# Last image of a four-layer vision block: half of its gate and output projection moved beside its scans, its first-layer input kept on the chip, filter products with wide weight tiles, ScalarE's copies shared

## The chip, the cores and the metric

The kernel runs on one core of a Trainium2 chip. The metric is the device time of one launch in microseconds (us). The engines named in what follows are TensorE (PE; its weight loads are listed as PEld), VectorE (DVE), ScalarE (ACT), GpSimd (POOL), and SyncE (SP), which issues the transfers; one queue of SyncE carries nearly all of them. SBUF is the memory on the chip with 128 partitions, PSUM the banks that TensorE writes into.

## The reference

Four images of 64 x 64 pixels with 96 channels pass through four layers, in float32 except where the feed-forward parts round to a small float format:

```python
x = x + mamba(group_norm(x))        # layer 0
x = depthwise_pointwise_conv(x)     # layer 1 (ReLU first, batch norm last)
t = tokens(x)                       # 4096 tokens of 96 channels
t = t + attention(ln(t))            # layer 2: six heads, no softmax
t = t + ffn(ln(t))                  # 96 -> 384 -> 96, rounded
t = t + filter(ln(t))               # layer 3
t = t + ffn(ln(t))

def mamba(x):
    xp, z = split(x @ W_in.T)                   # 192 channels each
    xc = silu(conv3x3(xp) + conv_b)
    # the same sequence by rows, by columns, and both reversed
    xs = four_orders(xc)
    dts, Bs, Cs = x_proj(xs)                    # 16 states
    delta = softplus(dt_proj(dts) + dt_b)
    # h = exp(delta*A)*h + delta*u*B ; y = sum(h*C) + D*u
    y = selective_scan(xs, delta, A, Bs, Cs, D)
    yy = y[0] + y[1] + y[2] + y[3]              # back in one order
    return (yy * silu(z)) @ W_out.T

def filter(x):
    h = relu(bn(x @ w1.T))                      # 96 -> 192
    X = fft(h, axis=tokens)                     # 4096 points
    xr = relu(X.real * rd - X.imag * id + rb)   # per channel
    xi = relu(X.imag * rd + X.real * id + ib)
    return bn(ifft(xr + 1j * xi).real @ w2.T)   # 192 -> 96
```

## The kernel before, in words

Channels lie on partitions and the 4096 positions of an image along the row, in eight blocks of 512. The kernel has a head, a scan stage and a tail.

**The head** (group norm, input projection and the 3 x 3 convolution of image 0) fills the inputs of the first scans. All such inputs go to DRAM tensors: step size, input product, B and C of the scans, `ud_s` (four times D times u) and `sz_s` (the gate, SiLU of z).

**The scan stage** has 192 phases: four images, each with two orientations (rows, columns), each with 24 groups of 8 channels x 16 states = 128 partitions. A phase takes one group through both directions in four chunks of 1024: ScalarE makes the decay (L1345), GpSimd multiplies by B (L1335), VectorE does four forward scans (L1568), four backward scans (L1611) and four adds (L1618), GpSimd multiplies by C (L1339), TensorE sums over the states (`py`, L1355), ScalarE copies (L1363), and the result goes to `y_s` in DRAM. For the column orientation ScalarE turns the inputs and the results by strided copies (L154) in a scratch tile `side`. The order within this stage is written out by hand. Eight times a phase `pieces` (L1421) gives pieces of other work to the engines, from two lanes. One lane has the scan inputs of images 1 to 3 and then `rest` of images 0 to 2; the other has the turns and `post` of images 0 to 2. Every piece states its cost on (PE, ACT, POOL, DVE, queue) in us; each step adds credit for each engine, and a piece goes out when there is credit for it.

**`post`** (L467) makes the first residual. For each block and each half of the 192 channels it loads three terms (the row result, `ud_s`, the turned-back column result), adds them in PSUM by products with the identity (`p_y`, L519), multiplies by the gate on VectorE (L494), projects by `w_out` (`p_out`, L546; two halves in one sum), adds x (L551), applies ReLU (L555) and stores `x1` to DRAM. For image 3 it runs after the last scan, with all eight PSUM banks.

**`rest`** (L698) has layers 1 to 3 of one image: `layer1` (nine taps, `p_l`, L753, from `x1` in DRAM), norms (`p_mean` L794, `p_var` L779, `p_rstd` L841), attention, a feed-forward, the filter, the last feed-forward (`p_f`, L960; copy L951, bias L953). Its argument `deep` is 1 beside the scans and 2 for image 3, which gives more buffers. Beside the scans the order is by hand; behind them the framework's scheduler orders what the lanes give, and helpers such as `evacuate` alternate between ScalarE and VectorE.

**The filter** writes the 4096 points as 64 x 64 and does the FFT as two steps of products with tables. `filter_in` (L1002) works on thirds of 64 channels. `p_h` (L1030) takes 64 columns of `ln`, every 64th element, as weights against `w1s`; it does each product twice, to partitions 0 to 63 and 64 to 127, so that both halves hold the same result. The gate `hb` (L1014) applies ReLU and a diagonal mask, and `p_dft` (L1051) takes 64 columns of `hb` at the same spacing against the real and the imaginary table, again in two column halves. The result `z` goes to DRAM (`z_s`) and comes back with other axes on the partitions. `filter_mid` (L1070) has 16 rounds of four frequencies: `p_dft2a` (L1107) with two thirds in two column halves, `p_dft2b` (L1116) with the last third, ReLU copies `ya` and `yb`, and the projection by `w2a` and `w2b` (`p_o`, L1090 and L1091). `filter_turn` (L1154) and `filter_out` (L1193) do the inverse.

The order of the tail is thus `post` of image 3, `layer1`, norm, attention, norm, feed-forward, norm, `filter_in`, `filter_mid`, `filter_turn`, `filter_out`, norm, feed-forward and output.

Of the kernel before, what the change touches and what calls it, by code (L numbers as in the profile page):

```python
# [10 lines left out]
F32 = mybir.dt.float32  # L11
# [7 lines left out]
NB = 4  # L19
# [54 lines left out]
def layers(ctx: ExitStack, tc: tile.TileContext, a: dict, out):  # L74
# [99 lines left out]
    def turn_back(side, b):  # L174

        yield from until(lambda: ("columns", b) in done)
        yield from turn(side, halves_of(y_s[1][b], y2_s[b]))

# [51 lines left out]
    def group_norm(wk, take, images, ready):  # L230
# [5 lines left out]
        for k, b in enumerate(images):  # L236
            stats = wk.tile([C, NBLK, 6], F32, tag="stats", name="stats", bufs=2)
            for i in range(NBLK):
                xs = wk.tile([C, BLK], F32, tag="xs", name="xs", bufs=4)
                nc.sync.dma_start(xs, a["xT"][:, b * L + i * BLK : b * L + (i + 1) * BLK])  # L240
                nc.vector.bn_stats(stats[:, i, :], xs)
                if i % 2 == 1 and n > 1:
                    yield NEXT
# [24 lines left out]
    def before_scans(b, wk, take, deep=1, prev=None):  # L268
# [109 lines left out]
        def k2(name, rows=C):  # L378
            return wk.tile([rows, BLK], F32, tag=name, name=name, bufs=2 * deep)

        soft = []
# [85 lines left out]
    def post(place, take, b, ahead):  # L467
# [3 lines left out]
        yield from until(lambda: ("scans", b) in done)  # L471

        def load(name, src, k):
            i, c = divmod(k, 2)
# [23 lines left out]
        def add_up():  # L498

            held = []  # L500
            for k in range(2 * NBLK):
# [22 lines left out]
                if k + 1 + ahead < 2 * NBLK:  # L524
                    yield (0, 0, 0, 0, 2.4)
                    nxt.append(load_terms(k + 1 + ahead))
                if k + 1 < 2 * NBLK and (k == 0 or k - 1 in used):
# [5 lines left out]
        for i in range(NBLK):  # L533
# [5 lines left out]
            for c in range(2):  # L539
                yield from until(lambda: 2 * i + c in sums)  # L540
                if c == 0:
                    p, give = yield from take("p_out")
                y, since = sums.pop(2 * i + c)
                yield from steps_past(since, 1)
                yield (0.9, 0, 0, 0)
                nc.tensor.matmul(p, lhsT=w_out[:, c, :], rhs=y, start=(c == 0), stop=(c == 1))  # L546
                used.add(2 * i + c)
# [6 lines left out]
            yield (0, 0.63, 0, 0, 1.6)  # L554
            nc.scalar.activation(xr, xr, AF.Relu)  # L555
            store(x1[b][:, cols], xr)
            yield NEXT
            flush()
            done["x1", b] = i + 1


    ident = mean_w = centre = pick = head_mask = dft1 = idft1 = taps = l1s = wk_a = wv_a = wqT = None
    bq = wff = bff = ffn2 = ffn3 = w1s = filt = imp = w2a = w2b = s2 = None

    def constants(wk, take, ready):

        nonlocal ident, mean_w, centre, pick, head_mask, dft1, idft1, taps, l1s, wk_a, wv_a, wqT
        nonlocal bq, wff, bff, ffn2, ffn3, w1s, filt, imp, w2a, w2b, s2
# [95 lines left out]
        w2a = const("w2a", [128, C], a["w2T"][0:128, :], cb)  # L664

        w2b = cb.tile([128, 2, C], F32, tag="w2b", name="w2b")
        nc.vector.memset(w2b, 0.0)
        for k in range(2):
            nc.sync.dma_start(w2b[k * N1 : (k + 1) * N1, k, :], a["w2T"][128:DI, :])
# [24 lines left out]

    def add_to(dst, src):
        (nc.gpsimd if ordered[0] else nc.vector).tensor_tensor(dst, dst, src, ALU.add)

    def rest(b, take, deep):  # L698
# [8 lines left out]
        def layer1(wk):  # L707
            x3 = x1[b].rearrange("p (r w) -> p r w", w=HW)

            def load(i):  # L710
                r0, lo, hi = rows_of(i)
                x = wk.tile([C, RPB + 2, HW], F32, tag="x", name="x", bufs=2)
# [51 lines left out]
        def layernorm(wk, hold, dst, source, result, previous=None):  # L764
# [3 lines left out]
            def half_of(h):  # L768
# [12 lines left out]
                def centred(i, pm, give):  # L781
# [3 lines left out]
                    nc.scalar.copy(hold[:, blk(i)], pm)  # L785
# [44 lines left out]
                def scale(i, pr, give):  # L830
                    kept = {} if dst.dtype == F32 else {"saturate": False}
                    nc.vector.tensor_tensor(dst[:, blk(i)], hold[:, blk(i)], pr, ALU.mult, **kept)  # L832
                    give(True)
                    ready[result] = i + 1
# [102 lines left out]
        def feed_forward(wk, weights, q, source, result, write=None):  # L937
# [4 lines left out]
            engine = nc.gpsimd if ordered[0] else nc.vector  # L942

            def first():
                for i in range(NBLK):
# [4 lines left out]
                    def out_of(j, p, give):  # L950
                        nc.scalar.copy(y[:, j, :], p)  # L951
                        give()
                        nc.scalar.activation(  # L953
                            y[:, j, :], y[:, j, :], AF.Relu, bias=b1[:, j : j + 1]
                        )
# [13 lines left out]
                    engine.tensor_copy(h, y, saturate=False)  # L969
                    hs[i] = h  # L970

            def second():
                for i in range(NBLK):
# [13 lines left out]
                    nc.scalar.copy(z, p)  # L987
                    give()
                    nc.scalar.activation(z, z, AF.Identity, bias=b2)
                    engine.tensor_tensor(t[:, blk(i)], t[:, blk(i)], z, ALU.add)  # L990
# [11 lines left out]
        def filter_in(wk, ln):  # L1002

            ln3 = ln.rearrange("p (n1 n2) -> p n1 n2", n2=N1)

            def third(hc):
                hs = slice(hc * N1, (hc + 1) * N1)
                yield from until(lambda: count("hb") >= hc)

                hb = wk.tile([128, N1, N1], F32, tag="hb", name="hb")  # L1010
                z = wk.tile([128, N1, N1], F32, tag="z", name="z")
# [11 lines left out]
                for k in range(8):  # L1023
                    p, give = yield from take("p_h", 128, held=held)
                    p = p.rearrange("p (n h) -> p n h", h=N1)
                    for j in range(8):
                        if j % 4 == 0:
                            yield (1.3, 0, 0, 0)
                        for at in (0, N1):
                            nc.tensor.matmul(  # L1030
                                p[at : at + N1, j, :], lhsT=ln3[:, :, 8 * k + j], rhs=w1s[:, hs],
                                start=True, stop=True,
                            )
                    yield from settle(held)
                    held.append(((0, 0, 0, 0.7), gate, (k, p, give), clock[0]))
                yield NEXT
                yield from settle(held)

                def out_of(k, p, give):
                    evacuate(z[:, :, 8 * k : 8 * k + 8], p.rearrange("p h k -> p k h"))  # L1040
# [3 lines left out]
                for k in range(8):  # L1044
                    p, give = yield from take("p_dft1", 128, held=held)
                    p = p.rearrange("p (h k) -> p h k", k=N1)
                    for j in range(8):
                        if j % 4 == 0:
                            yield (1.3, 0, 0, 0)
                        for ri in range(2):  # L1050
                            nc.tensor.matmul(  # L1051
                                p[ri * N1 : (ri + 1) * N1, j, :], lhsT=hb[:, :, 8 * k + j],
                                rhs=dft1[:, ri, :], start=True, stop=True,
                            )
# [6 lines left out]
                for q in range(4):  # L1061
                    yield (0, 0, 0, 0, 2.1)
                    nc.sync.dma_start(
                        z_s[b][:, hc, chunk(q)], z.rearrange("p k c -> p (k c)")[:, chunk(q)]
                    )

            for hc in range(3):
                yield from third(hc)
# [676 lines left out]
```

## Time and profile before

The median is 6014.21 us, of three runs from 6010.89 to 6023.8. The profiled execution spans 6031.1 us.

| engine | busy us | share of the span | instructions |
|---|---|---|---|
| TensorE, products | 4284.0 | 71% | 19506 |
| TensorE, weight loads | 1848.1 | 31% | 19506 |
| VectorE | 4864.0 | 81% | 3492 |
| ScalarE | 3283.7 | 54% | 4452 |
| GpSimd | 4077.9 | 68% | 1961 |

By stretches of the span (busy us):

| stretch, us | what | PE | PEld | VectorE | ScalarE | GpSimd |
|---|---|---|---|---|---|---|
| 0 to 360 | head | 322.3 | 121.4 | 34.2 | 197.8 | 80.0 |
| 360 to 5469 | scans | 3475.2 | 1424.3 | 4696.0 | 2920.9 | 3991.2 |
| 5469 to 5543 | `post` of image 3 | 62.7 | 21.3 | 15.9 | 5.6 | 6.0 |
| 5543 to 5731 | `layer1` to first feed-forward | 164.9 | 58.2 | 43.6 | 88.2 | 0.6 |
| 5731 to 5847 | `filter_in` | 113.1 | 112.5 | 25.4 | 7.2 | 0 |
| 5847 to 5861 | way of `z` through DRAM | 3.2 | 2.8 | 1.0 | 0.6 | 0 |
| 5861 to 5916 | `filter_mid` | 54.3 | 50.1 | 12.7 | 11.4 | 0 |
| 5916 to 6031 | turn, inverse, norm, last feed-forward | 88.4 | 57.5 | 35.3 | 52.1 | 0 |

A row is read against its own length: an engine that is busy for nearly the whole stretch bounds it. Products and weight loads of TensorE overlap, so the two columns do not add up. PEclk in the lines of the profile is the granted clock of TensorE as a share of full speed; it differs between stretches, and so does the time of one product.

### The profile page before, as it was taken

How to read it: one execution, taken by the hardware profiler on the slowest of the kernel's cores; microseconds unless marked ns; L12 is line 12 of the kernel's file. 1: busy time of each engine (PE TensorE's matmuls, PEld its weight loads, DVE VectorE, ACT ScalarE, POOL GpSimd, SP SyncE). 2: the span in 40 equal slices, each digit the busy share in tenths (PEclk: the TensorE clock that was granted, in tenths of full speed). 3: DMA queues.
4: the chain of work that ended last, by engine and by line, in shares of the span. 5: the costliest groups of instructions: out<-in, count | busy, mean ns of one | idle time of the engine just before them, and what ended most of it. 6: DMA issues, size and time to landing. Idle time of an engine off the chain costs nothing. (4 is left out here: it accounts for less than half of the span.)

```text
span 6031.1 us, 64385 instructions
## 1 busy us (share of the span) xinstructions
PE 4284.0 (71%) x19506; PEld 1848.1 (31%) x19506; DVE 4864.0 (81%) x3492; ACT 3283.7 (54%) x4452; POOL 4077.9 (68%) x1961
## 2 busy tenths in 40 slices
PE   8978888889855774654577756675577566657888
PEld 3322222223211120343412203551122044512285
DVE  2058898898899899998899999999989999993222
ACT  4557767776663357555454465455435645461503
POOL 1268897898897668777677787777767877782000
PEclk9988888888866765566657755685776557757787
DMA  3268878876788868789978677786875588854021
GB/s 100 75 165 232 238 199 231 242 230 196 207 246 233 221 193 224 215 232 252 251 211 227 178 201 215 212 246 187 233 203 162 169 234 235 231 163 130 4 82 56
DMA packets 467624, 1170.28 MB, mean 194 GB/s; under 512 B 90240, under 2 KB 155372, under 8 KB 467180
## 3 DMA queue, kind: packets, MB, share of 16 engines
q1 hardware_dynamic: 467276, 1166.17, 69.6%
q8 instruction: 154, 2.52, 0.2%
q14 instruction: 194, 1.59, 0.1%
HBM read 1010.63 MB, written 155.19 MB: 193 GB/s over the span
## 5 line engine op out<-in xcount | busy, mean ns | idle before, releaser
L1339 POOL TENSOR_TENSOR S<-S,rep 128x1024 f32<-128x1024 f32 x768 | 1811.1, 2359 | 942.1 <-DVE S L1618 863.3
L1345 ACT ACTIVATE pa<-dl,nega 128x1024 f32<-128x1024 f32 x1344 | 1500.3, 1118 | 1470.1 <-DVE S L1618 1121.8
L1335 POOL TENSOR_TENSOR B<-B,rep 128x1024 f32<-128x1024 f32 x768 | 1795.0, 2366 | 73.7 <-DMA B<-duT_s 50.6
L1568 DVE TENSOR_TENSOR_SCAN S<-pa,S,B 128x1024 f32<-128x1024 f32 x576 | 1352.6, 2348 | 261.8 <-ACT pa L1345 67.6
L1611 DVE TENSOR_TENSOR_SCAN pa<-pa,edge,B 128x1024 f32<-128x1024 f32 x576 | 1354.4, 2351 | 66.8 <-ACT pa L1345 66.7
L1355 PE MATMUL py<-S,red 128*32 128x512 f32 x3072 | 632.9, 890 | 820.1 <-POOL S L1339 746.2
L359 PE MATMUL p_conv<-xp,conv_w 96*96 96x504 f32 (+3 forms) x2304 | 1059.9, 615 | 14.9 <-ACT u L372 12.9
L1618 DVE TENSOR_TENSOR S<-S,pa 128x1024 f32<-128x1024 f32 x768 | 932.1, 1214 | 6.6
L359 PEld LDWEIGHTS p_conv<-xp,conv_w 96*96 96x96 f32 x2304 | 387.2, 171 | 673.4 <-issue 619.0
L1568 DVE TENSOR_TENSOR_SCAN S<-pa,B 128x1024 f32<-128x1024 f32 x192 | 438.1, 2282 | 178.9 <-ACT pa L1345 178.4
L1611 DVE TENSOR_TENSOR_SCAN pa<-pa,B 128x1024 f32<-128x1024 f32 x192 | 440.9, 2296 | 5.4
L1355 PEld LDWEIGHTS py<-S,red 128*32 128x32 f32 x3072 | 76.0, 128 | 1189.3 <-POOL S L1339 972.2
L154 ACT COPY side<-side 96x256 f32<-96x256 f32 (+1 forms) x448 | 281.7, 629 | 62.3 <-DMA duT_s<-side 28.8
L794 PE MATMUL p_mean<-t,centre 96*96 96x512 f32 x256 | 207.3, 929 | 118.0 <-ACT sq L786 46.9
L753 PE MATMUL p_l<-x,taps 96*96 96x504 f32 (+3 forms) x576 | 268.9, 623 | 16.0 <-DMA x<-x 16.0
L1051 PE MATMUL p_dft<-dft,hb 128*64 128x64 f32 x3072 | 231.3, 320 | 59.4 <-DVE hb L1014 59.4
L1030 PE MATMUL p_h<-w1s,ln 97*64 97x64 f32 x3072 | 233.6, 342 | 35.2 <-DVE ln L832 20.6
L1030 PEld LDWEIGHTS p_h<-w1s,ln 97*64 97x64 f32 x3072 | 227.7, 251 | 79.3 <-issue 33.3
L1051 PEld LDWEIGHTS p_dft<-dft,hb 128*64 128x64 f32 x3072 | 227.2, 251 | 79.7 <-DVE hb L1014 63.0
L451 POOL TENSOR_TENSOR r<-r,lg 96x512 f32<-96x512 f32 x64 | 81.3, 1271 | 250.0 <-ACT lg L436 249.9
L1363 ACT COPY ys<-py 128x512 f32<-128x512 f32 x384 | 221.8, 578 | 22.4 <-PE py L1355 19.8
L841 PE MATMUL p_rstd<-rs_y,pick 32*96 32x512 f32 x256 | 169.5, 1004 | 70.4 <-DVE ln L832 23.6
(192 smaller groups left out, 5081.9 us busy)
## 6 DMA issues: line engine op xcount, KB each, us to landing
B<-du_s SPq DMA_DIRECT2D x768, 256.0 KB
dl<-delta_s SPq DMA_DIRECT2D x768, 256.0 KB
B<-duT_s SPq DMA_DIRECT2D x768, 256.0 KB
dl<-deltaT_s SPq DMA_DIRECT2D x768, 256.0 KB
z_s<-z SPq DMA_DIRECT2D x48, 512.0 KB
zl<-z_s SPq DMA_DIRECT2D x64, 384.0 KB
side<-y_s SPq DMA_DIRECT2D x96, 192.0 KB
rep<-bc_s SPq DMA_DIRECT2D x64, 256.0 KB
```

The source lines that it names most:

```text
L154: nc.scalar.copy(o.rearrange("p (w h) -> p w h", h=HW), t[:n, :].rearrange("p (h w) -> p w h", w=HW)[:, q * w : (q + 1) * w, :],)
L359: nc.tensor.matmul(pr[:, ra:rb, ca_:cb_], lhsT=conv_w[:, kc, ky * 3 + kx, oc * C : (oc + 1) * C], rhs=xp[:, kc, at + ra : at + rb, ca_ + d ...
L753: nc.tensor.matmul(p3[:, ra:rb, ca_:cb_], lhsT=taps[:, ky * 3 + kx, :], rhs=x[:, at + ra : at + rb, ca_ + dx : cb_ + dx], start=(k == 0), ...
L1030: nc.tensor.matmul(p[at : at + N1, j, :], lhsT=ln3[:, :, 8 * k + j], rhs=w1s[:, hs], start=True, stop=True,)
L1051: nc.tensor.matmul(p[ri * N1 : (ri + 1) * N1, j, :], lhsT=hb[:, :, 8 * k + j], rhs=dft1[:, ri, :], start=True, stop=True,)
L1335: nc.gpsimd.tensor_tensor(Bs[n, q], Bs[n, q], reps[n // NG, 0, q], ALU.mult)
L1339: nc.gpsimd.tensor_tensor(Ss[n, q], Ss[n, q], reps[n // NG, 1, q], ALU.mult)
L1345: nc.scalar.activation(pa, dls[n, q], AF.Exp, scale=nega[:, g : g + 1])
L1355: nc.tensor.matmul(py[32 * j : 32 * j + 32, :], lhsT=red, rhs=Ss[n, q][:, k * BLK : (k + 1) * BLK], start=True, stop=True,)
L1568: nc.vector.tensor_tensor_scan(s, pa, Bs[n, q], Ss[n, q - 1][:, CH - 1 : CH] if q else 0.0, ALU.mult, ALU.add)
L1611: nc.vector.tensor_tensor_scan(pa[:, ::-1], pa[:, ::-1], Bs[n, q][:, ::-1], edge if k else 0.0, ALU.mult, ALU.add,)
L1618: nc.vector.tensor_tensor(Ss[n, q], Ss[n, q], pa, ALU.add)
```

## The change

It has four parts.

1. *Half of gate and projection beside the scans.* The channels 0 to 95 of the last image have all four scan results once group 12 of its last orientation is through. So the side lane gets, at its end, a `post` of this half alone (`halves=(0,)`), whose result (with x, before ReLU) is stored to `x1`. For the channels 96 to 191 `sum_up` adds `ud_s` and the turned-back column results in advance and stores the sum to `ud_s`. The last phase loads these sums, the gates and the partial `x1` into tiles that the scans no longer need (`last_loads`). Behind the scans `last_post` loads only the row results of the upper half, adds, gates, projects, adds and applies ReLU.
2. *`x1` of the last image kept on the chip.* `last_post` writes it into the scratch tile `side`, and `layer1` reads it there. `side` is now allocated from the start, and some tiles of the head (`xs`, and `w`, `lg` of image 0) use its space.
3. *Filter products of 128 weight columns.* In the tail `ln` is written twice, side by side (the copy on GpSimd), so that `p_h` is one product with 128 weight columns and writes both halves at once. `p_dft` takes a pair of columns of `hb` as 128 weight columns against both tables side by side (128 moving columns), for all images. The thirds of the tail's `filter_in` are given to the scheduler as three parallel streams with two sets of buffers. `z` gets another layout; `filter_mid` loads it by four transfers a round and takes 96 weight columns of two half sets, 16 bytes from one to the next, each for all its channels; `ya`, `yb` are replaced by two tiles of 96 partitions, and the projection has two products with 96 rows for each frequency.
4. *Copies shared in the tail.* In the feed-forward parts copies and biases alternate between ScalarE and VectorE (`evacuate`, `plus_bias`); the copy `hold` of a norm goes to VectorE; the cast to eight bits goes to GpSimd.

The core of the diff:

```diff
+            if 1 in halves:
+                yield (0, 0.63, 0, 0)
+                nc.scalar.activation(xr, xr, AF.Relu)
...
+    def sum_up(place, take, b):
...
+            p, give = yield from take("p_sum", C, held=held)
+            yield (1.6, 0, 0, 0)
+            for j, x in enumerate(terms):
+                nc.tensor.matmul(p, lhsT=ident[:C, :C], rhs=x, start=(j == 0), stop=(j == 1))
...
+    def last_post(place, take, x1t):
+        b = NB - 1
+        for i in range(NBLK):
+            nc.sync.dma_start(place("y_in", i), y_s[0][b][C:, i * BLK : (i + 1) * BLK])
+        for i in range(NBLK):
+            cols = slice(i * BLK, (i + 1) * BLK)
+            y, w, sz, xr = (place(name, i) for name in ("y_in", "w_in", "sz_in", "xr"))
+            (nc.gpsimd if i % 2 else nc.vector).tensor_tensor(y, y, w, ALU.add)
+            nc.vector.tensor_tensor(y, y, sz, ALU.mult)
+            p, give = yield from take("p_out")
+            nc.tensor.matmul(p, lhsT=w_out[:, 1, :], rhs=y, start=True, stop=True)
+            nc.vector.tensor_tensor(xr, p, xr, ALU.add)
+            give()
+            nc.scalar.activation(x1t[:, cols], xr, AF.Relu)
...
+    def plus_bias(x, bias, relu=False):
+        if ordered[0] or not flip[0]:
+            nc.scalar.activation(x, x, AF.Relu if relu else AF.Identity, bias=bias)
+        elif relu:
+            nc.vector.tensor_scalar(x, x, bias, 0.0, ALU.add, ALU.max)
+        else:
+            nc.vector.tensor_scalar(x, x, bias, None, ALU.add)
...
+                    if result == "ln_s" and deep > 1:
+                        nc.gpsimd.tensor_copy(
+                            dst[:, L + i * BLK : L + (i + 1) * BLK], dst[:, blk(i)]
+                        )
...
-                        nc.scalar.copy(y[:, j, :], p)
+                        evacuate(y[:, j, :], p)
...
-                    engine.tensor_copy(h, y, saturate=False)
+                    nc.gpsimd.tensor_copy(h, y, saturate=False)
...
-                        for at in (0, N1):
+                        for at in (0,) if deep > 1 else (0, N1):
                             nc.tensor.matmul(
-                                p[at : at + N1, j, :], lhsT=ln3[:, :, 8 * k + j], rhs=w1s[:, hs],
-                                start=True, stop=True,
+                                p[at : at + deep * N1, j, :], lhsT=ln3[:, :, 8 * k + j],
+                                rhs=w1s[:, hs], start=True, stop=True,
...
-                        for ri in range(2):
-                            nc.tensor.matmul(
-                                p[ri * N1 : (ri + 1) * N1, j, :], lhsT=hb[:, :, 8 * k + j],
-                                rhs=dft1[:, ri, :], start=True, stop=True,
-                            )
+                    for j in range(4):
+                        nc.tensor.matmul(
+                            p[:, j, :], lhsT=pairs[:, :, 4 * k + j], rhs=table,
+                            start=True, stop=True,
+                        )
...
-                        for hc in range(2):
+                        for j in range(4):
                             nc.tensor.matmul(
-                                pa[hc * N1 : (hc + 1) * N1, j, :], lhsT=z[:, hc, j, :],
-                                rhs=tw[:, j, :], start=True, stop=True,
+                                p[:, j, :], lhsT=z[:, c, :, j], rhs=tw[:, j, :],
+                                start=True, stop=True,
                             )
...
+            if n == N - NG // 2 + 1:
+                done["half", NB - 1] = True
...
+    x1t = side[:, :L]
+    drain([*lanes, Lane(iter([([last_post(last_place, take, x1t)], [])]))])
```

## Prediction, made before the changed kernel had run

> **What bounds the kernel now.** I read the busy time by stretches first, then the chain of work that ended last, then the groups of instructions by line, and last the weight loads of the lines that the change rewrites.
>
> ```profile
> core 0: us, PE busy (x) PEld busy (x) DVE busy (x) ACT busy (x) POOL busy (x), PEclk, DMA share, GB/s
> 4500.00:5200.00 700.00, 448.09 (x2976) 237.96 (x2978) 660.94 (x464) 371.27 (x496) 531.68 (x247) 0.66 0.74 205
> 5455.00:5530.00 75.00, 63.60 (x135) 21.40 (x136) 27.18 (x31) 7.19 (x10) 9.91 (x5) 0.80 0.67 195
> 5650.00:5750.00 100.00, 79.69 (x390) 33.38 (x388) 33.08 (x48) 61.98 (x113) 0.00 (x0) 0.66 0.00 1
> 5750.00:5850.00 100.00, 94.44 (x1284) 93.84 (x1282) 20.52 (x31) 7.17 (x12) 0.00 (x0) 0.85 0.13 50
> 5850.00:5940.00 90.00, 81.28 (x1024) 76.62 (x1024) 16.70 (x30) 15.59 (x30) 0.00 (x0) 0.92 0.41 134
> ```
>
> There are two regimes. From 360 to 5469 us VectorE is full (94% in the first stretch shown): every phase has eight scans and four adds, 24.4 us in phases without other VectorE work. What VectorE gets besides lengthens a phase one for one; TensorE has room. From 5469 to 6031 (562 us) image 3 is alone and TensorE carries it, with its weight loads as busy as its matmuls where the filter products run.
>
> ```profile
> 5469.20 2.35 POOL S L1339
> ...
> 5543.15 48.92 PE p_l L753 x108
> ...
> 5731.40 18.91 PE p_h L1030 x253
> 5751.08 18.92 PE p_dft L1051 x256
> ...
> 5860.65 1.98 PE p_dft2a L1107 x16
> 5865.47 1.02 PE p_dft2a L1107 x16
> 5868.88 1.02 PE p_dft2a L1107 x16
> ...
> 5915.82 24.04 PE p_idft L1154 x384
> ```
>
> This is the chain: start, length, work. The tail divides into: gate and projection, 5469 to 5543 (74 us); first layer, norms, attention and feed-forward to 5731; `filter_in`, three times 18.9 + 18.9, 115.5 us; the way of `z` through memory to 5860.6; `filter_mid`, 16 rounds of 3.42, 55 us; the rest to the end.
>
> ```profile
> L1051 PEld LDWEIGHTS p_dft<-dft,hb x256: 217/251/257, 5751.1 to 5769.6; 128*64 128x64 f32 x128
> L1107 PEld LDWEIGHTS p_dft2a<-tw,zl x182: 132/137/137, 5872.2 to 5910.0; 128*64 128x64 f32 x182
> L1090 PEld LDWEIGHTS p_o<-w2a,ya x96: 186/192/192, 5870.3 to 5909.3; 128*128 128x128 f32 x96
> L154 ACT COPY side<-side x448: 607/624/1035, 396.1 to 5031.5; 96x256 f32<-96x256 f32 x128, 32x256 f32<-32x256 f32 x22
> ```
>
> Durations are minimum, median, maximum in ns. A load of 64 columns that lie side by side takes 132, of 128 such columns 186: (186 - 132) / 64 = 0.84 ns a column on 78 fixed. The same 64 columns taken 256 bytes apart (`p_dft`) take at least 217: 139 / 64 = 2.2 ns a column. ScalarE shows the same kind of thing: 624 ns for 256 elements read 256 bytes apart.
>
> [...] two passes of `p_dft`, one in each half of the columns, start 7 ns apart and a pair comes every 147 ns; between `p_dft2a` (two tiles) and `p_o` (one) lie about 0.2 us, twice a round.
>
> So the old pairs already used both halves of the array. What a single tile of 128 spaced columns costs, no row shows. Bounds: packed, 112 ns a pass (the step of `p_o`); at 2.2 ns, 128 x 2.2 + 6 = 287. The single records tell more: where the last load of a burst runs on after its partner, it shortens by about 0.2 ns per ns alone (lead 98 ns: 229 instead of 251), so a stream alone needs about 2.2 / 1.2 = 1.8 ns a column, and not half of 2.2. Sharing one supply would have shortened it by nearly the whole lead. With 1.67 to 1.84 a pass is 218 to 240; I take 228.
>
> **The change part by part.**
>
> *Half of gate and projection beside the scans; `x1` on the chip.* The eight gates and eight adds of the lower 96 channels move into the last phases: 16 x 0.68 = 10.9 us of VectorE, which is full there. The order of instructions puts 236.4 us of such side work before the end of the scans instead of 228.3 (+8; four casts of image 2 slip behind). `sum_up` costs VectorE nothing (16 products, 8 ScalarE copies of 0.58, 24 transfers, beside the scans). More transfers in the queue of the loads: +2. Scans: +10. Behind the scans, before: 74 us to the first `p_l`. After: product 2.4, `py` 2.0, copy 0.6, store and load back 6: first inputs 11 us after the scans, all eight by 18. VectorE then has 4 adds, 8 products and 8 adds, 20 x 0.69 = 13.8. But the order also leaves four to five blocks of image 2's last feed-forward here, ahead of `p_l` in TensorE's queue: 4 casts, 9 copies and 8 biases, 13 us more on VectorE. 27 us of VectorE from the end of the scans with a few us of waits: `p_l` at +30 instead of +74, so -44. From there `p_l` is bound by TensorE as before.
>
> *ScalarE's copies shared.* A feed-forward block costs ScalarE 4.35 us now (steady, no gaps):
>
> ```profile
> L953 ACT ACTIVATE y<-y,b_L 128x512 f16<-128x512 f16 x48 | 33.2, 737 | 0.0
> L951 ACT CAST y<-p_f 128x512 f16<-128x512 f32 x48 | 26.7, 598 | 10.3 <-PE p_f L960 10.3
> ```
>
> These are groups of the tail: busy, mean ns, idle before. After, ScalarE has half (2.2) and VectorE two copies (1.38), two biases on 16-bit data (no row; between 0.3, at the rate of the cast `h<-y`, 0.62 ns an element, and 0.69), the add (0.69), and in the last layer the scaling (0.68): about 3.5. The cast goes to GpSimd, 1.46 for 0.96, beside the next block. 8 x 0.85 = 7 for the last layer, and 1 from its norm: -8. In the second layer norms are interleaved [...]: -10. The copy of `ln` on GpSimd (bounded by its 1.27 for a two-input product of that size) lags VectorE's 0.68 over four blocks: +3 before `p_h` can start.
>
> *`filter_in`.* Of `p_h` 64 x 2 = 128 passes a third instead of 128 pairs: 128 x 0.228 = 29.2 us for 18.9. Of `p_dft` 32 x 2 = 64 passes: 14.6 for 18.9. Three thirds: 131.4 + 4 for the waits that stay (the order still runs `p_h` and `p_dft` of a third one after the other) = 135 for 115.5: +19. Images 0 to 2 change only `p_dft`, in TensorE's room: nothing.
>
> *`filter_mid`.* Eight products of 96 columns, 16 bytes apart, in 16 passes: 96 x 1.75 + 5 = 173 ns [...]. I take 170: 2.7 us; `p_o` stays at 16 x 0.112 = 1.8[...]. 4.5 for 3.42, over 16 rounds: +17. Four loads for one: +1 before the first round; the bytes are the same, 655 KB a round, beside 4.5 us.
>
> *Head.* `xs`, `w`, `lg` only change place: 0, hidden by TensorE's 161 of 180 us there.
>
> Sum: +10 - 44 - 8 - 10 + 3 + 19 + 17 + 1 = -12, so 6002 from 6014; I say 6000.
>
> **The rivals.**
> A. *A column 16 bytes from the next costs no more than a packed one.* For it: nothing measured[...]. `filter_mid` then +2 instead of +17: 5985. 0.17.
> B. *One wide tile loads spaced columns at near the packed rate.* Then `p_h` and `p_dft` take 112 to 150 ns a pass: 69 to 90 us for 115.5, and the tail wins about 55 more than I say: 5930. For it: two streams together deliver a column every 1.1 ns. Against it: the lone loads at the end of the bursts. 0.12.
> C. *Slower: the wide load keeps 2.2 ns a column, or the scans pay more.* 287 a pass: 192 x 3 x 0.059 = 34 more than I have. Or TensorE's fuller rounds and the five transfers a round hold up the scans, 20 us or more: SyncE issues a load in about 0.54 us, and 64 more per image stand before the loads of the scans; the planner books 0.9 for four `p_dft` products that take 1.8. Against it: phases 80 to 86 and 124 to 139 of before show next to no wait besides VectorE's own work. 6035. 0.16.
>
> **How the numbers follow.** My case, 0.55, spreads over 5985 to 6018: 218 or 240 a pass moves it by -6 and +7, biases and waits behind the scans by 8, the scans by 8. Range 5940 to 6035: it leaves out a good part of B and the upper part of C, under 0.2 together. Faster by over 0.2% (below 6002): about half of my case, A and B: 0.58. Slower (over 6026): 0.17. The same: 0.25.
>
> **What would show it.** Right: the first `p_l` about 30 us behind the last scan; weight loads of `p_h` near 300 ns where now 217 to 257 stand; `p_h` at 29 us and the tail's `p_dft` at 15 us a third; rounds of `filter_mid` at 4.5 us; last feed-forward blocks near 3.5 us apart; scans longer by about 10 us. Wrong: `p_h` under 20 us a third (B), rounds of 3.6 (A), `p_h` over 35 or scans longer by over 25 (C).

## The result, and the profile after

The changed kernel takes 6096.76 us (median; 6092.45 to 6110.99) where the kernel before takes 6018.26 beside it. The ratio is 1.0135, with a 95% interval of 1.0114 to 1.0157: it is slower by about 80 us. The forecast was 6000, faster, with a range up to 6035.

The stretches of the changed kernel (start and end, length, then busy time and number of instructions of PE, PEld, DVE, ACT and POOL, granted clock, share of the transfer engines, GB/s):

```profile
360.00:5543.00 5183.00, 3502.95 (x13337) 1451.37 (x13337) 4700.05 (x3205) 2908.54 (x3854) 3969.46 (x1874) 0.71 0.77 215
5543.00:5593.00 50.00, 29.75 (x57) 8.75 (x55) 36.61 (x43) 15.24 (x25) 28.07 (x18) 0.57 0.21 63
5593.00:5767.00 174.00, 151.66 (x459) 56.15 (x457) 70.55 (x114) 62.84 (x106) 18.96 (x23) 0.89 0.01 3
5767.00:5895.00 128.00, 126.28 (x576) 125.90 (x576) 25.56 (x39) 7.16 (x12) 0.00 (x0) 0.65 0.08 33
5905.00:5979.00 74.00, 74.00 (x512) 73.95 (x510) 14.89 (x23) 13.40 (x24) 0.00 (x0) 0.98 0.45 131
6029.00:6090.00 61.00, 40.92 (x98) 12.49 (x96) 37.98 (x61) 28.63 (x48) 12.66 (x8) 0.67 0.09 26
```

The tail, from the end of the last scan on, is 547 us where it was 563: shorter, as forecast. The scan stage, from the first scan to the end of the last, is 5186 us where it was 5107, with VectorE as busy as before (4700 against 4696 us). So VectorE does not have more to do there; it waits. These are two single executions: that of the kernel before took 15 us more than its median, that of the changed kernel 4 us less. So between these two profiles the scan stage is 79 us longer and the whole only some 60, while the medians differ by 79; by the medians the scan stage's excess is nearer 95 us. 79 is used below. The chain of the tail (start, length, work):

```profile
5592.75 47.89 PE p_l L834 x108
...
5798.57 14.08 PE p_dft L1141 x64
5812.65 27.85 PE p_h L1119 x128
5840.50 14.08 PE p_dft L1141 x64
...
5912.75 2.85 PE p_dft L1204 x16
5915.60 1.76 PE p_o L1186 x16
```

A third of `p_h` takes 27.85 us (18.9 before), a third of `p_dft` 14.08 (18.9), a round of `filter_mid` 2.85 + 1.76 = 4.61 (3.42). The weight loads behind these numbers (minimum, median, maximum in ns):

```profile
L1141 PEld LDWEIGHTS p_dft<-dft,hb x768: 291/313/316, 2501.0 to 5893.6; 128*128 128x128 f32 x192
L1204 PEld LDWEIGHTS p_dft<-tw,zl x1024: 250/274/284, 2696.1 to 5975.1; 128*96 128x96 f32 x171
```

The wide loads cost about what the forecast took: 14.08 / 64 = 220 ns a pass (I took 228), 2.85 / 16 = 178 (I took 170).

For the scan stage I set each phase against its content: 24.39 us for the scans and adds, the measured VectorE side work, and the rest as stall. Summed over 191 phases, side work grew from about 320 to 328 us (+8, the number of the forecast), and stalls from about 106 to 177 (+71). The new stalls lie in three places: phases 78 to 99 (filter of image 0), 124 to 141 (image 1), and from 168 to the end (image 2, and the new half). The waits of ScalarE on filter products over the scan stage show how they come about, first before the change, then after (engine, what waited, for what: us in total, times, longest):

```profile
ACT z L689 <- PE p_dft L1051: 64.2, 49, 4.5
ACT os L689 <- PE p_o L1091: 42.0, 26, 4.5
ACT ya L689 <- PE p_dft2a L1107: 20.7, 16, 3.0
```

```profile
ACT z L758 <- PE p_dft L1141: 76.0, 51, 5.9
ACT y L758 <- PE p_dft L1204: 55.3, 30, 7.6
ACT os L758 <- PE p_o L1186: 40.3, 32, 3.3
```

ScalarE waits 172 us for products of the filter instead of 127. Decays `pa` of the next scans stand behind the waiting copies in its order of work. VectorE's own waits for `pa` in the scan stage, without the wait for the very first one, grew from about 140 us to 214. One phase of image 1 shows it: before, the phase at 3779.5 us had 68 records (one a pass) of `p_h` and 178 of `p_dft`; after, that at 3832.7 has 219 of `p_h` and 40 of the wide `p_dft`. The lines are before, then after:

```profile
3779.50:3805.00 25.50, 21.41 (x266) 18.52 (x265) 25.36 (x21) 11.48 (x14) 18.87 (x8) 0.73 0.58 170
```

```profile
3832.70:3866.30 33.60, 27.30 (x273) 25.25 (x270) 27.90 (x24) 11.39 (x13) 25.18 (x12) 0.59 0.73 229
```

TensorE is busy longer, but that alone does not make the 33.6 us: it also stands idle for 6.29 us in this phase, before `p_dft`, until VectorE has done a gate `hb` between its scans. Then the products come. Every copy waits for eight passes, 1.76 us; four copies stand in a row, the first decay of the next phase comes after them, and VectorE waits for it (start, length, engine, line and operation; in brackets the idle time before, and what ended it):

```profile
3861.26 0.60 ACT L758 ACTIVATE z<-p_dft 128x512 f32<-128x512 f32 x1 [1.16 <-PE p_dft L1141]
3863.00 0.60 ACT L758 ACTIVATE z<-p_dft 128x512 f32<-128x512 f32 x1 [1.15 <-PE p_dft L1141]
3864.65 0.60 ACT L758 ACTIVATE z<-p_dft 128x512 f32<-128x512 f32 x1 [1.05 <-PE p_dft L1141]
3865.14 1.11 ACT L1443 ACTIVATE pa<-dl,nega 128x1024 f32<-128x1024 f32 x1
3866.34 2.29 DVE L1668 TENSOR_TENSOR_SCAN S<-pa,B 128x1024 f32<-128x1024 f32 x1 [5.61 <-ACT pa L1443]
```

### The profile page after: what moved, and what is told of

The parts are those of the page before. It is cut to its first block, busy times and chain, and to the rows that moved or that the text cites. A ratio compares the mean times of both kernels' runs of the same rounds, so it can differ in the third digit from the quotient of the medians.

```text
span 6090.1 us, 58316 instructions
## 1 busy us (share of the span) xinstructions
PE 4290.0 (70%) x16290; PEld 1893.7 (31%) x16290; DVE 4936.8 (81%) x3600; ACT 3240.3 (53%) x4347; POOL 4112.5 (68%) x1989
## 3 DMA queue, kind: packets, MB, share of 16 engines
q14 instruction: 196, 1.61, 0.1%
## 5 line engine op out<-in xcount | busy, mean ns | idle before, releaser
L1055 POOL CAST h<-y 128x1536 fp8e5<-128x1536 f16 x64 | 95.6, 1494 | 409.7 <-ACT y L767 388.1
L1119 PE MATMUL p_h<-w1s,ln 97*64 97x64 f32 (+1 forms) x2688 | 260.0, 353 | 30.0 <-DVE ln L916 18.0
L1119 PEld LDWEIGHTS p_h<-w1s,ln 97*64 97x64 f32 (+1 forms) x2688 | 254.8, 259 | 68.8 <-issue 30.0
L527 PE MATMUL p_y<-side,ident 96*96 96x512 f32 x336 | 215.0, 791 | 26.6 <-DMA side<-y_s 11.5
L1204 PE MATMUL p_dft<-tw,zl 128*96 128x128 f32 x1024 | 209.5, 372 | 27.3 <-DMA tw<-in_dft 16.3
L1204 PEld LDWEIGHTS p_dft<-tw,zl 128*96 128x96 f32 x1024 | 198.5, 274 | 74.9 <-issue 44.3
```

The costliest lines, as they stand in the source:

```text
L1119: nc.tensor.matmul(p[at : at + deep * N1, j, :], lhsT=ln3[:, :, 8 * k + j], rhs=w1s[:, hs], start=True, stop=True,)
L1204: nc.tensor.matmul(p[:, j, :], lhsT=z[:, c, :, j], rhs=tw[:, j, :], start=True, stop=True,)
```

## The experiments

Three theories were set against each other.

1. *Prices.* The planner of the scan stage (the credits by which `pieces` gives out work) books 0.9 us for four `p_dft` products, which are eight passes of 220 ns, 1.76 us; and 1.1 + 1.1 + 1.6 = 3.8 for a round of `filter_mid` that takes 4.61. The old prices were 1.3 for 1.18 and 5.6 for 3.42. So the planner now gives the products out faster than TensorE makes them. (The rounds are those of the tail, at a granted clock of 0.98. In the scan stage it is 0.71 in the mean: in the changed kernel's stretches where the granted clock is 0.5 a pass of `filter_mid`'s `p_dft` comes every 213 ns and not 177, one of `p_o` every 213 and not 112, while `filter_in`'s `p_dft` stays at 220.)
2. *Transfers.* The five transfers of a round, four of them of 96 KB in pieces of 512 bytes, hold up the loads of the scans.
3. *The half.* Gate, projection and sums beside the last scans cost more than their VectorE time.

All ratios are against the kernel before the change on the same chip, with 95% intervals. The scan stage, from the first to the last scan, is read from the profiles. It also varies from one execution to another: with the old products, prices and loads it was 5091 to 5107 us in three kernels (before the change, e6, e11), and e8, with the scan stage of the changed kernel, had 5203 where that had 5186. So a difference of under some 17 us in it says nothing by itself.

**e1, prices raised to the old margin.**

```diff
-                    yield (0.9, 0, 0, 0)
+                    yield (1.9, 0, 0, 0)
...
-                        yield (1.1, 0, 0, 0, 0 if c else 2.6)
+                        yield (2.3, 0, 0, 0, 0 if c else 2.6)
...
-                    yield (1.6, 0, 0, 0)
+                    yield (2.9, 0, 0, 0)
```

> The changed kernel, with only the three prices at which the planner gives out the filter's products beside the scans raised so that booked over real is as before the change (four p_dft products 1.9 instead of 0.9, four second-step products 2.3 instead of 1.1, the projection 2.9 instead of 1.6). Theory 1 (under-priced products put more on TensorE than a phase holds, ScalarE waits for them in order, its decays come late and the scans with them): the scan stage, 71 us of stalls longer than before, gives back 35 to 65 us, total 6035 to 6062. Theory 2 (the five short-pieced transfers a round hold up the loads of the scans): they only spread, under 20 us come back, total 6077 to 6097. Theory 3 (the half of gate and projection and the sums beside the last scans): within 10 us of 6097.

Measured: 6083.29 us, ratio 1.0115 (1.0091 to 1.0139). The total missed the range of theory 1 and lies in that of theory 2. The scan stage gave back 31 us (5186 to 5155), just under the 35 to 65 of theory 1 and more than theory 2 allowed, and the waits of ScalarE on filter products fell to 116 us, below those of before the change. But 14 us came back behind the scans: with dearer products image 2 ends later, more of its last feed-forward stands ahead of image 3, and the first `p_l` came 63 us behind the last scan instead of 49. Prices are one cause; this run leaves room for others.

**e4, the kernel before the change with halved prices.** No product, transfer or layout differs.

```diff
-                            yield (1.3, 0, 0, 0)
+                            yield (0.65, 0, 0, 0)
...
-                    yield (2.4, 0, 0, 0, 2.6)
+                    yield (1.2, 0, 0, 0, 2.6)
...
-                    yield (0.8, 0.6, 0, 0)
+                    yield (0.4, 0.6, 0, 0)
...
-                    yield (2.4, 0, 0, 0)
+                    yield (1.2, 0, 0, 0)
```

> The kernel before the change, with nothing changed but the prices of p_dft, of the second step and of the projection, halved (1.3 to 0.65, 2.4 to 1.2, 0.8 to 0.4, 2.4 to 1.2). No product, transfer or layout differs. Theory 1: the old products, too, then come in bunches that a phase cannot hold, and the scan stage gets 25 to 70 us longer: 6040 to 6085. Theory 2 and 3: within 10 us of before, 6005 to 6028.

Measured: 6080.89 us, ratio 1.0108 (1.0086 to 1.0131). Theory 1 holds: four numbers that do no work cost 63 us by the medians; in the profiles the scan stage grows by 53 (5107 to 5160). The waits of ScalarE there:

```profile
ACT z L689 <- PE p_dft L1051: 112.2, 64, 6.4
ACT os L689 <- PE p_o L1091: 45.1, 30, 3.2
ACT ya L689 <- PE p_dft2a L1107: 30.6, 17, 4.5
```

The wait for `p_dft` went from 64 to 112 us with the very same products. What the prices changed is the order on ScalarE, and not how much a phase can hold: a phase of this kernel with 256 records of `p_dft` is 29.1 us long, while the kernel before has one with 256 as well that takes 24.4, at the same VectorE work (before, then e4):

```profile
2581.60:2606.00 24.40, 21.09 (x272) 19.20 (x272) 23.44 (x16) 16.23 (x23) 19.12 (x8) 0.90 0.80 214
3861.90:3891.00 29.10, 22.05 (x272) 19.27 (x272) 23.67 (x17) 12.76 (x17) 18.88 (x8) 0.79 0.49 148
```

In the first, at most two copies of `z` stand between two decays, and no scan waits for a decay. In the second, four do, from 3869.38 to 3878.05 us, three of them waiting 2.90, 1.75 and 1.74 us for their products, and VectorE then waits 2.66 us for the decay behind them.

**e7, the price of `p_dft` alone halved** (the first edit of e4).

> The kernel before the change with the price of p_dft alone halved (1.3 to 0.65). If filter_in makes most of what the four halved prices cost (63 us): 6045 to 6065. If filter_mid does: 6020 to 6035.

Measured: 6068.23 us, ratio 1.0077 (1.0063 to 1.0090): 47 of the 63 us by the medians, 3 above the range of the first case. In the profiles the scan stage is as long as in e4 (5158 and 5160 us). So most of it is `filter_in`, where the bookings of the change are also furthest off (0.9 for 1.76).

**e5, the kernel before the change with each load of `z` split in four.**

```diff
-                nc.sync.dma_start(
-                    z.rearrange("p h k c -> p h (k c)"), z_s[b][:, :, k0 * N1 : (k0 + 4) * N1]
-                )
+                for ri in range(2):
+                    for c in range(2):
+                        at = (k0 + 2 * c) * N1
+                        nc.sync.dma_start(
+                            z[ri * N1 : (ri + 1) * N1, :, 2 * c : 2 * c + 2, :].rearrange("p h k c -> p h (k c)"),
+                            z_s[b][ri * N1 : (ri + 1) * N1, :, at : at + 2 * N1],
+                        )
```

> The kernel before the change with one thing altered: each load of z for a round of filter_mid is four transfers of 96 KB in pieces of 512 bytes, as in the changed kernel, instead of one of 384 KB in pieces of 1024. Products and prices stay. Theory 2 (transfers): the rounds' phases get stalls of 1 to 5 us as in the changed kernel, total 6030 to 6050. Theory 1: within 8 us of before. The raised prices left some 20 us of the scans' loss in the filter's phases, and this run tells whether the transfers are that rest.

Measured: 6061.0 us, ratio 1.0065 (1.0052 to 1.0078). Theory 2 holds as well, and costs more than it was given. The longer phases are those of `filter_mid`: phases 134 to 137 were 24.4 to 25.4 us long and are 25.9 to 33.3, the phases around them are as before. The stretch of image 1's `filter_mid` in the kernel before and here:

```profile
3896.00:4042.00 146.00, 101.01 (x1083) 81.60 (x1084) 138.92 (x89) 78.59 (x114) 112.47 (x48) 0.85 0.90 250
```

```profile
3910.00:4077.00 167.00, 116.54 (x1120) 96.18 (x1120) 144.10 (x94) 80.58 (x118) 114.42 (x50) 0.79 0.90 223
```

The transfer engines are 0.90 busy in both, but move 223 GB/s instead of 250. TensorE's wait for the table `tw`, the last transfer of a round, over the same two stretches:

```profile
PE p_dft2a L1107 <- DMA tw<-in_dft: 4.5, 3, 3.2
```

```profile
PE p_dft2a L1111 <- DMA tw<-in_dft: 32.6, 10, 7.6
```

**e9 and e12, the number and the pieces apart.** e9 loads `z` in three transfers, one for each third, in pieces of 1024 bytes; e12 in two, in pieces of 512.

```diff
+                for hc in range(3):
+                    nc.sync.dma_start(
+                        z[:, hc].rearrange("p k c -> p (k c)"),
+                        z_s[b][:, hc, k0 * N1 : (k0 + 4) * N1],
+                    )
```

```diff
+                for c in range(2):
+                    at = (k0 + 2 * c) * N1
+                    nc.sync.dma_start(
+                        z[:, :, 2 * c : 2 * c + 2, :].rearrange("p h k c -> p h (k c)"),
+                        z_s[b][:, :, at : at + 2 * N1],
+                    )
```

> The kernel before the change with each load of z for a round of filter_mid as three transfers of 128 KB, one for each third, in pieces of 1024 bytes as before; e5 had four of 96 KB in pieces of 512 and lost 0.65%. If the number of transfers is what holds up the scans: about two thirds of that loss, 6040 to 6052. If the short pieces are: 6015 to 6028.

> The kernel before the change with each load of z for a round of filter_mid as two transfers of 192 KB in pieces of 512 bytes: the pieces of e5, with half its transfers. If the short pieces are what costs (the transfer engines are 0.90 busy in that stretch either way, and moved 223 instead of 250 GB/s in e5): most of the loss of e5 stays, 6040 to 6060. If it takes the four transfers: 6010 to 6026.

Measured: e9 1.0003 (0.9995 to 1.0011), e12 0.9998 (0.9989 to 1.0007). Neither costs anything that the times show, though in both one phase of image 1 (number 136) is 28.4 us long where it was 24.4. Each expectation had pointed to the other's cause: pieces of 512 bytes alone are not it, and three transfers are not either. e5 differs from both in one more way, for each of its transfers fills 64 partitions and not 128; no run has that alone in the kernel before. Two readings of e5 remain. SyncE takes about 0.6 us to issue one of e5's transfers, and in the stretch above it is issuing for 59% of the time before and for 72% in e5. Or it is the way the program counts transfers: SyncE's go through eight semaphores in turn (6240 issues in the kernel before, 780 on each), an issue waits until the one eight places earlier has landed (so with all 62 waits for a landing in the stretch above, before), and five transfers a round leave three places for the scans. The traces speak for the first. Over these two stretches, of 15 rounds each, SyncE's issuing grew from 86 to 120 us, while its waits for landings, which the counting would lengthen, fell from 43 to 33. By the median of one issue, the loads of `z` cost SyncE 0.55 us a round before, 1.29 in e9, 1.11 in e12, and 2.42 in e5 (1.08 in e10, below). This is read from traces and not shown by a run that changes one alone.

**e10, the changed kernel with raised prices and the four loads merged into two.**

```diff
-                    for c in range(2):
-                        nc.sync.dma_start(
-                            z[ri * N1 : (ri + 1) * N1, c].rearrange("p (h j) k -> p h (j k)", h=3),
-                            z_s[b].rearrange("(n c) h q -> c n h q", c=2)[c, :, :, at : at + 4 * 32],
-                        )
+                    nc.sync.dma_start(
+                        z[ri * N1 : (ri + 1) * N1].rearrange("p c (h j) k -> p (c h) (j k)", h=3),
+                        z_s[b].rearrange("(n c) h q -> n (c h) q", c=2)[:, :, at : at + 4 * 32],
+                    )
```

> The changed kernel with raised prices (as e1) and with the four loads of a round merged into two of 192 KB; the pieces stay at 512 bytes. If prices and the number of transfers together are the scans' loss in the filter's phases: the 20 us that e1 left there mostly go, 6060 to 6072. If short pieces are the second cause: within 8 us of e1, 6075 to 6090.

Measured: 6059.48 us, ratio 1.0073 (1.0059 to 1.0088), 24 us below e1 and within 1 us of the first case. The scan stage is 5138 us: of the 79 us that the change added to it, prices and number of transfers together give back 48. The intervals of e1 and e10 do not meet; between their profiles the scan stage differs by 16 us, of which about 8 lie in the filter's phases and 7 in phases 182 to 190. The merged loads still fill 64 partitions each, so it is not that alone which held up e1. About 17 of the other 31 lie in phases 182 to 190, where the half is; the rest is near the run-to-run spread.

**e2, old filter for all images.** Products, prices, layout and loads of the filter are those before the change; the half, `x1` on the chip and the shared copies stay.

> The changed kernel with the filter products, their prices, the layout of z and its loads as before the change, for all four images; half of the last image beside its scans, x1 on the chip and the shared copies stay. Theory 1 and 2: the stalls of images 0 and 1 go, the scan stage is longer than before by 8 to 25 us only (the side work of VectorE and what the half costs), and the tail keeps its gains without the filter's loss: 5960 to 5995. Theory 3: the scan stage stays 50 to 80 us longer than before; 6030 to 6070.

Measured: 6011.11 us, ratio 0.9987 (0.9979 to 0.9996). The scan stage fell to 5124 us, as theories 1 and 2 have it, but the total stayed 16 us above their range. Seven blocks of image 2's feed-forward were left behind the scans, and the first `p_l` came 62 us after the last scan.

**e3, without the half and without `x1` on the chip.**

```diff
-        steps += [sum_up(place, take, 3), post(place, take, 3, 1, (0,))]
...
-    drain([*lanes, Lane(iter([([last_post(last_place, take, x1t)], [])]))])
+    drain([*lanes, Lane(iter([([post(last_place, take, NB - 1, 3)], [region])]))])
...
-    drain([Lane(tail(x1t, aside))])
+    drain([Lane(tail(None, None))])
```

> The changed kernel without the half beside the scans and without x1 on the chip: the whole gate and projection of the last image behind its last scan, as before; the wide products and the shared copies stay. Theory 1 and 2: the scans of images 0 and 1 stay as in the changed kernel, the last stretch (phases 175 to 191) gives back at most 25 us, the first p_l comes about 72 us behind the last scan instead of 46: 6085 to 6125. Theory 3: the scan stage gives back 50 to 75 us: 6050 to 6075.

Measured: 6108.56 us, ratio 1.0150 (1.0130 to 1.0169). Theory 3 falls as the main cause: the stalls of images 0 and 1 stay. Phases 182 to 190 give back 18 us (256 to 237), and the first `p_l` comes at +73 instead of +49. The two nearly cancel: the interval overlaps that of the changed kernel.

**e6, shared copies alone** (the edits of e2 and e3 together).

> Old filter products for all images, whole gate and projection behind the last scan, x1 through DRAM; only the shared copies, biases and casts of the tail stay of the change. If the half costs the scans about as much as it saves behind them: 5996 to 6006. If the half is worth the 12 us that leaving it out of the changed kernel cost: 6018 to 6026.

Measured: 6002.31 us, ratio 0.9970 (0.9959 to 0.9981), as the first case has it. It is 0.17% below e2, which has the half and `x1` on the chip besides; the two intervals touch.

**e8, the tail's `p_h` in pairs again, in the changed kernel.**

```diff
-                        for at in (0,) if deep > 1 else (0, N1):
+                        for at in (0, N1):
                             nc.tensor.matmul(
-                                p[at : at + deep * N1, j, :], lhsT=ln3[:, :, 8 * k + j],
+                                p[at : at + N1, j, :], lhsT=ln3[:, :, 8 * k + j],
```

> The changed kernel with p_h of the tail as pairs of 64 columns again, and ln written once. From the traces (a third of p_h 18.9 us in pairs, 27.9 with 128 columns): filter_in 27 us shorter, total 6065 to 6075. If the wide weight loads cost nothing that TensorE does not also lose elsewhere (waits for the gate take their place): 6085 to 6097.

Measured: 6070.93 us, ratio 1.0083 (1.0067 to 1.0099), 26 us below the changed kernel, as the loss by wide loads in the chain has it: 3 x (27.85 - 18.9) = 27. The profiles say it more exactly. From the first `p_h` to the first product of `filter_mid` it takes 109.6 us here, 137.6 in the changed kernel and 126.1 before: the wide `p_dft` and the parallel thirds win 16 us, and the wide `p_h` loses 28. A wide `p_dft` halves the number of passes (64 of 220 ns for 128 pairs of 147); a wide `p_h` only puts 128 passes of 218 in place of 128 pairs. Behind the scans `ln` written once wins another 5 us, up to the first `p_l` (+44.5 for +49.4); the scan stage of this execution was 17 us longer.

**e11, e6 with `x1` of the last image kept on the chip.**

```diff
-                nc.scalar.activation(xr, xr, AF.Relu)
-            yield (0, 0, 0, 0, 1.6)
-            store(x1[b][:, cols], xr)
+                nc.scalar.activation(xr if x1t is None else x1t[:, cols], xr, AF.Relu)
+            if x1t is None:
+                yield (0, 0, 0, 0, 1.6)
+                store(x1[b][:, cols], xr)
```

> As e6 (old filter products, whole gate and projection behind the scans, shared copies), and x1 of the last image goes into the scratch tile on the chip instead of to DRAM and back. If the way through DRAM stands on the path to the first p_l, some 4 to 8 us come off e6 (6002): 5993 to 5999. If the gate and projection bound it anyway: 6000 to 6005.

Measured: 5982.81 us, ratio 0.9950 (0.9936 to 0.9963): faster than both kernels, and by more than expected; by the ratios e11 is 12 us below e6, where 4 to 8 were expected. The first `p_l` is 64 us behind the last scan instead of 72 in e6, and from there to `p_h` it takes 171 us instead of 174.

```profile
5447.00:5511.00 64.00, 62.24 (x134) 21.68 (x133) 16.89 (x25) 4.99 (x8) 5.98 (x5) 0.88 0.72 193
```

TensorE is busy for 62 of these 64 us, where it was busy for 63 of 74 before the change: with `x1` on the chip, its own work fills this stretch.

e11 and e2 differ in the half alone. e2 is at 0.9987 and e11 at 0.9950, with intervals that do not meet: with the old filter the half costs 0.37%, some 22 us. It brings the first `p_l` no nearer (62 us behind the last scan for 64), since blocks of image 2's feed-forward stand ahead of it, and phases 182 to 190 take 260 us for 238.

## Why the prediction was wrong

**The step that failed** is the sentence that images 0 to 2 change only `p_dft`, in TensorE's room: nothing. By the work the change is small: an image's three thirds of `p_dft` get 15 us shorter and its rounds of `filter_mid` 19 us longer. But room over the stage is not room at the moment when a copy waits. The planner hands out work by its prices. The change books a third of `p_dft` at 7.2 us instead of 20.8, while its time fell only from 18.9 to 14.1, and a round of `filter_mid` at 3.8 instead of 5.6, while its time rose from 3.42 to 4.61. With the old products, wrong prices alone cost 63 us (e4), and four transfers in place of one cost 40 (e5). The two do not add up in the changed kernel, whose whole excess in the scans is 79 us; raising the prices and merging the transfers gives back 48 of it (e10). I had named both, the 0.9 for 1.8 and the five transfers, in rival C, gave them "20 us or more", and set against them that those phases of the kernel before show next to no wait. (Its "64 more" loads per image are 64 in place of 16, so 48 more.) That was no evidence: with the old prices halved and all else the same, the waits come (e4). The waits of one profile did not tell how near the stage was to them; the bookings beside the measured durations could have.

**The scans' other terms.** VectorE's side work is +8, as worked out. The +2 for more transfers was mis-sized: phases 182 to 190 take 18 us more with the half (e3), 8 of it side work and 10 stalls. What makes these stalls no run shows.

**Behind the scans.** I had the first `p_l` at +30; it comes at +49, a gain of 26 instead of 44. With the old filter `x1` on the chip alone wins 9 of such a gain (e6 to e11). VectorE is busy 36.6 us there instead of 27. The gates took 0.97 us in the median (up to 1.75) where I had 0.69, and one bias took 6.05:

```profile
L771 DVE TENSOR_SCALAR z<-z,b_L x18: 335/348/6052, 5570.2 to 6082.9; 96x512 f16<-96x512 f16 x18
```

**Shared copies.** From the first `p_l` to `p_h` it takes 174 us instead of 188: 14 less, where I had 10 less 3. The end from `filter_out` on is 5.5 us shorter, where I had 8.

**The filter of the tail.** The wide weight load was right: 220 ns a pass for 228, 178 for 170. (That columns 16 bytes apart would cost about what those 256 bytes apart do was my estimate; no row of before showed it.) From the first `p_h` to the first product of `filter_mid` it takes 11 us more instead of 20, since a third of `p_h` and `p_dft` take 42 instead of 44 us and the waits between thirds went. `filter_mid`, from there to `p_idft`, takes 17 more, as I had: its rounds cost 19, and 2 of waiting at its start went. Rivals A and B fall: with columns 16 bytes apart a pass takes 178 ns where the packed `p_o` takes 112, and a wide tile loads 128 spaced columns in 291 to 316 ns where 128 packed ones take 186. In all, the tail is 16 us shorter, where the terms behind the scans gave 22. The sum failed in the main in one place, the scan stage.

What is left open: by experiment, whether SyncE's issue time or the eight places in flight make e5's four transfers dear; what stalls the phases beside the half; and 14 of the 31 us that e10 leaves in the scan stage.

## What to carry to other kernels

Where a planner hands out work by booked costs, a change of an operation is a change of its price too. Check booked over measured for each piece, before and after, since a stage without waits can lie just below the point where waiting copies pile up ahead of the work that the bounding engine needs. Try each part of a change alone too: here `x1` on the chip with the shared copies was 0.5% faster, and the other parts took that back. Read a change beside a full stage by phases and by the order on each queue, the time to issue transfers included, and not by free time over the whole stage.

## What the hardware showed that was not expected

VectorE's bias on 16-bit data takes 0.34 us and took 6.05 once, while GpSimd filled the row of ones of `ln` from 5579.8 to 5586.7 us; it ended with the fill, at 5586.9. It came again: 5.59 us in e1 and 5.76 in e10, beside the same fill, and 2.63 in e8, beside the short one. A cast on VectorE that reads PSUM took its usual 0.69 us within the fill. That fill is itself a cost of the change: with `ln` twice as wide it takes 6.92 us instead of 3.51. Nine other biases of the changed kernel began while GpSimd ran a cast; they took 0.68 to 1.61 us and ended 0.14 to 0.22 us after the cast. The bias beside the fill ended 0.15 us after it. So in this trace each such bias lasted until GpSimd's instruction ended; what held it is not shown.

Splitting a load in three, or in two with pieces half as long, cost nothing (1.0003 and 0.9998); splitting it in four, by partitions too, cost 0.65%, beside transfer engines that were 0.88 to 0.90 busy in all four kernels.
